# A four-layer graph network on one core: layer 1's inverse sums on ScalarE, its features by nodes, its first exponents inside layer 0

## The chip, the cores and the metric

The kernel runs on one core of a Trainium2 chip. A core has a tensor engine (PE) for matrix products and transposes, VectorE (DVE), ScalarE (ACT) and GpSimd (POOL), each with its own queue of instructions that it works through in order, and SyncE (SP), which issues DMAs here. PE writes to PSUM, eight banks of 2 KB a partition; everything else is in SBUF. The metric is device microseconds of one execution. The three runs before the change took 2126.72 us in the median (2126.08 to 2129.75).

## The reference, cut to what matters

Sixteen graphs share one adjacency matrix of 1024 nodes, each node has 64 features, and everything is float32. Four layers follow each other, each as `x = layernorm(x + layer(x))`. Layers 0 and 2 are graph attention with one score per edge, layer 3 has four heads. Layer 1, which the change is about, has a softmax of its own for each feature:

```python
feat = softplus(x * (INV_SQRT2 * w0) + b0)            # [16, 1024, 64]
scores = feat * wa + ba                               # wa, ba: one value per feature
logits = where(adj > 0, scores[:, None], -1e9)
attn = softmax(logits, axis=2)                        # over the neighbours j
out = einsum('bijd,bjd->bid', attn, feat)
x = layernorm(x + out)
```

Since the score depends on the neighbour alone, out is a quotient of two products with the adjacency matrix: adj @ (exp(score) * feat) over adj @ exp(score). The scores may be shifted by any constant per graph and feature, which cancels.

## The kernel before, in words

`fast_path` computes everything with shifts that fit ordinary data and collects tests of its bounds in `flags` (function `check`, L1750 to L1755). At the end a register is loaded from the smallest flag, and only if a test failed `general_path` computes everything again. One of the tests concerns `most_var`, the largest variance met in any layer norm, which is final only late in layer 3.

A node lies on partition p and in block c of 8 (`C`): x is held as `xg[g]`, [128 partitions, 8 blocks, 4 graphs, 64 features], for four groups g of four graphs. Two graphs side by side give 128 columns, a "pair"; q numbers the two pairs of a group.

**Layer 0** (`gat_layer`, L884 to L1142) works through the graphs in steps (b, k): batch b, node block k. At each step VectorE makes the weights `e` of one block (L964), PE multiplies those of four steps earlier (L976, L988), and further tasks hang on steps through the table `slots`: evictions, projections (L1016, L1020), division (L1033 to L1045), statistics, and the preparation of later graphs, whose product `pg` (L944) uses a PSUM pool `ps_g` with a single buffer of two banks. Tasks of other parts are hung on steps through the dictionary `extra`. The layer is issued under a manual schedule: each engine's order is the order written. What is outside such a block is ordered by the framework's planner, which fills in where it takes an engine to be idle: in the trace some of the checks (L1752, L1754) run in the middle of layer 0, and transposes of layer 2 (L903) among layer 1's products.

`gat_layer` returns the tasks left over at its end, `ending`: projection, division, residual, statistics, root and shift of batch 15, and the rows ("store") of batches 14 and 15, eight small ScalarE operations each (L775).

**Layer 1** follows (L1498 to L1607), outside a manual schedule. The adjacency is copied to `aR` in the type of the fast single-pass float32 product (L1512, eight casts). For each group, `prep_l1` makes the values. Per pair: eight transposes put features on partitions (L1522); ScalarE computes |z|, exp(-|z|), max(z, 0) and log(1+exp(-|z|)) (L1524 to L1528) and VectorE adds them (L1529): the softplus. Still with features on partitions, VectorE takes the maximum of feat*wa over the nodes (L1536) and from it the shift `down` (L1539), ScalarE makes the exponents (L1540), VectorE multiplies them by the features (L1541). Then both results are transposed back (`halves`, L1550, two times eight), and each is split in two numbers `hi` (a cast on ScalarE, L1552) and `lo` (the remainder, VectorE, L1553), so that two fast products give nearly full precision.

`product_l1` (L1567) forms for a group and a node block ic the sixteen products over the neighbours' blocks into one PSUM bank `po`, of a pool with two: quotient's numerator and denominator of both pairs. `average` (L1574 to L1582) divides and adds:

```python
nc.vector.reciprocal(r, po[:, :, 1, :])
nc.vector.tensor_tensor(r, po[:, :, 0, :], r, ALU.mult)
...
nc.vector.tensor_tensor(yf, r.rearrange("p q f -> p (q f)"), yf, ALU.add)
```

and takes the statistics of the layer norm. In the loop over groups (L1588 to L1607) each node block is followed by a task of the next group's preparation and one of the last group's normalization (`root`, `shift`, and `scaled` rows on ScalarE, 32 small operations a group). The preparation of group 0 runs before the first product, between the first three tasks of `ending`.

**The start**: SP's queue loads the first two graphs, the adjacency in eight pieces (four buffers), two more graphs, the weights of layers 2 and 3, the other twelve graphs, and then the six small pieces of layer 1's parameters `w0`, `b0`, `wa`, `ba`.

## Time and profile before

| What | Value |
|---|---|
| runs, median | 2126.72 us (2126.08 to 2129.75) |
| profiled execution | 2126.6 us, span 2124.7 us, mean PE clock 0.974 |
| layer 0's last product ends | 283.6 us |
| layer 1's products (L1567) | 308.5 to 448.3 us |
| busy in the span | PE 1998.2, VectorE 1858.1, ScalarE 1228.0, GpSimd 55.6 us |

The profile's page comes from one execution. A busy share is an average over stages that have different limits, so stretches of time and the chain of work that ended last have to be read beside it. In a row of groups, "mean ns of one" is the length of one instruction, and the last part tells how long its engine stood idle before it and what ended that. Rows of one engine overlap a little, so the spacing of starts is somewhat less than the length.

### The profile page before, as it was taken

The page shows a single profiled execution, that of the slowest core. Times are in us where ns is not written, and L with a number is a line of the kernel's source. Part 1 is how long each engine was busy: PE and PEld are TensorE (multiplying, and loading weights), DVE is VectorE, ACT ScalarE, POOL GpSimd, SP SyncE. Part 2 cuts the span into 40 slices and gives each one's busy share as a digit, 9 for nine tenths or more (in the row PEclk, how much of TensorE's full clock was granted, in tenths as well). Part 3 has the DMA queues.
Part 4 walks back from the last instruction along what each step waited for, and adds up shares of the span by engine and source line. Part 5 has one row for each costly group of instructions (what it writes and reads, how often), then busy time and mean ns, then how long its engine had stood idle before and what let it go on. Part 6 is the DMA issues. An engine that isn't in the chain of part 4 may idle for free.

```text
span 2124.7 us, 26159 instructions
## 1 busy us (share of the span) xinstructions
PE 1998.2 (94%) x10065; PEld 845.2 (40%) x10065; DVE 1858.1 (87%) x3224; ACT 1228.0 (58%) x1965; POOL 55.6 (3%) x77
## 2 busy tenths in 40 slices
PE   7999979988898999999999999999999999999993
PEld 3444447753332333333333333333333333333331
DVE  5888989989999867898888898889889889889997
ACT  4355566555556756556656655655665666565541
POOL 0000000000000000000000000000000000000001
PEclk7999989999989999999999999999999999999997
DMA  6000000000000100000000000000000000000000
GB/s 165 1 1 1 1 1 1 1 0 1 1 1 31 50 1 1 1 1 6 6 1 6 1 6 6 1 6 1 6 6 1 6 1 6 6 1 6 6 6 12
DMA packets 23654, 18.89 MB, mean 9 GB/s; under 512 B 19361, under 2 KB 19426, under 8 KB 23522
## 3 DMA queue, kind: packets, MB, share of 16 engines
q1 hardware_dynamic: 23218, 17.11, 2.7%
q8 instruction: 81, 1.33, 0.3%
q14 instruction: 51, 0.42, 0.1%
q10 hardware_dynamic: 304, 0.03, 0.0%
HBM read 12.95 MB, written 4.19 MB: 8 GB/s over the span
## 4 chain that ended last, share of the span: by engine, by line
PE 68%; DVE 26%; ACT 4%; issue 1%; DMA 0%; POOL 0%; SPq 0%; POOLq 0%; DVEq 0%; ACTq 0%
PE y L1293 19%; PE s L1281 17%; DVE e L964 7%; PE y_l L976 6%; PE s L1378 5%; PE y L1405 4%; DVE e L1286 4%; PE po L1310 3%; PE u_l L988 3%; PE po L1567 3%; ACT e L1285 1%; DVE r L1576 1%; PE pzT L1339 1%; PE phT L1255 1%; DVE junk L1396 1%
## 5 line engine op out<-in xcount | busy, mean ns | idle before, releaser
L1285 ACT ACTIVATE e<-s,shift 128x1024 f32<-128x1024 f32 x512 | 542.8, 1111 | 242.8 <-PE s L1281 237.4
L1286 DVE TENSOR_TENSOR e<-e,aT 128x1024 f32<-128x1024 f32 x512 | 602.5, 1220 | 87.2 <-ACT e L1285 85.1
L1281 PE MATMUL s<-hT 64*128 64x512 f32 x2048 | 508.9, 610 | 16.0 <-DVE top L1222 8.8
L1293 PE MATMUL y<-e,vals 128*64 128x512 f32 x2048 | 490.6, 601 | 3.2 <-ACT yT L1300 1.3
L964 DVE SCALAR_TENSOR_TENSOR e<-G_l,q,aT 128x1024 f32<-128x1024 f32 x256 | 315.4, 1278 | 7.2 <-ACT G_l L945 7.2
L976 PE MATMUL y_l<-e,vals_l 128*64 128x512 f32 x1024 | 263.6, 639 | 23.8 <-DVE e L964 23.0
L1281 PEld LDWEIGHTS s<-hT 64*128 64x128 f32 x2048 | 181.8, 186 | 256.3 <-issue 169.2
L1293 PEld LDWEIGHTS y<-e,vals 128*64 128x64 f32 x2048 | 131.0, 136 | 330.6 <-issue 257.7
L1383 ACT ACTIVATE e<-s,shift 128x1024 f32<-128x1024 f32 x128 | 141.7, 1112 | 84.8 <-PE s L1378 74.9
L1385 DVE TENSOR_TENSOR me<-e,aT 128x1024 f32<-128x1024 f32 x128 | 155.8, 1220 | 16.8 <-ACT e L1383 16.5
L1396 DVE SCALAR_TENSOR_TENSOR junk<-e,aN 128x1024 bf16<-128x1024 f32 x128 | 156.0, 1219 | 0.2
L1405 PE MATMUL y<-me,h2v 128*64 128x512 f32 x512 | 135.3, 609 | 10.6 <-DVE me L1385 10.4
L1378 PE MATMUL s<-h2T 64*128 64x512 f32 x512 | 136.3, 610 | 4.6 <-DVE h2v L1365 4.4
L976 PEld LDWEIGHTS y_l<-e,vals_l 128*64 128x64 f32 x1024 | 65.6, 142 | 162.2 <-issue 75.0
L1567 PE MATMUL po<-hi,aR 128*128 128x512 f32 x256 | 101.9, 398 | 2.7 <-ACT hi L1552 1.1
L1567 PE MATMUL po<-lo,aR 128*128 128x512 f32 x256 | 99.8, 390 | 0.0
L775 ACT ACTIVATE x<-m,bn_shift,bn_rstd 128x64 f32<-128x64 f32 x256 | 88.2, 429 | 0.0
L1340 ACT COPY zT<-pzT 128x1024 f32<-128x1024 f32 x32 | 32.4, 1013 | 78.4 <-PE pzT L1339 78.4
L1310 PEld LDWEIGHTS po<-wb,yT 128*128 128x128 f32 x512 | 62.0, 190 | 34.0 <-issue 21.1
L1310 PE MATMUL po<-wb,yT 128*128 128x130 f32 x512 | 73.8, 287 | 1.3 <-ACT e L1285 1.2
L1378 PEld LDWEIGHTS s<-h2T 64*128 64x128 f32 x512 | 46.6, 186 | 63.7 <-issue 41.4
L1405 PEld LDWEIGHTS y<-me,h2v 128*64 128x64 f32 x512 | 32.7, 137 | 93.8 <-issue 56.1
(214 smaller groups left out, 2003.7 us busy)
## 6 DMA issues: line engine op xcount, KB each, us to landing
adj<-in_adj_dram SPq DMA_DIRECT2D x16, 512.0 KB, 4.5
x<-in_x_dram SPq DMA_DIRECT2D x16, 256.0 KB, 5.0
out_dram<-res SPq DMA_DIRECT2D x16, 256.0 KB, 2.0
wl<-in_L_gnn_Wh_dram SPq DMA_DIRECT2D x2, 64.0 KB, 4.8
wo<-in_L_gnn_Wo_dram SPq DMA_DIRECT2D x1, 64.0 KB, 4.4
l_wd<-in_L_gnn_W_dram ACTq DMA_DIRECT2D x2, 16.0 KB, 4.7
l_wd<-in_L_gnn_W_dram SPq DMA_DIRECT2D x2, 16.0 KB, 2.1
bo<-in_L_gnn_bo_dram SPq DMA_DIRECT2D x1, 32.0 KB, 3.1
```

The costliest lines, as they stand in the source:

```text
L964: nc.vector.scalar_tensor_tensor(e, G[b - b % 2][:, b % 2, :], pq[b - b % 2][1][:, k, b % 2 : b % 2 + 1], aT[:, k, :], ALU.max, ALU.mult,)
L976: nc.tensor.matmul(held["y"][h * D : (h + 1) * D, :], vals[b][:, k, :], e[:, h * HALF : (h + 1) * HALF], start=(k == 0), stop=(k == C - 1),)
L1281: nc.tensor.matmul(s[:, i, :], hT[rows, k * P : (k + 1) * P], hT[rows, cols], start=True, stop=True)
L1285: nc.scalar.activation(e, s, AF.Exp, bias=shifts[b, n])
L1286: nc.vector.tensor_tensor(e, e, bc_mid(aT[:, k, cols], 2), ALU.mult)
L1293: nc.tensor.matmul(held[h][i * D : (i + 1) * D, :], vals[b][:, k, :], e[:, i, :], start=(k == 0), stop=(k == C - 1),)
L1310: nc.tensor.matmul(o[:, j // 2, j % 2, :], held["y"][:, c * P : (c + 1) * P], wb[:, n, :], start=True, stop=True,)
L1378: nc.tensor.matmul(s[:, i, :], hT[rows, (i + k // CH) % 2, k % CH * P : (k % CH + 1) * P], hT[rows, 0, :], start=True, stop=True,)
L1385: nc.vector.tensor_tensor(m, e, aT[:, k, :].rearrange("p (i q) -> p i q", i=2), ALU.mult)
L1396: nc.vector.scalar_tensor_tensor(junk, held.pop(k).rearrange("p i q -> p (i q)"), 1.0, aN[:, k, :], ALU.mult, ALU.mult, accum_out=sums[:, ...
L1405: nc.tensor.matmul(held["o"][h * D : (h + 1) * D, :], vals["out", b][:, k, :], e[:, h, :], start=(k == 0), stop=(k == C - 1),)
L1567: nc.tensor.matmul(po.rearrange("p q k f -> p (q k f)"), aR[:, k, ic * P : (ic + 1) * P], e[:, k].rearrange("p q k f -> p (q k f)"), start ...
```

## The change

Four things change. First, in `average` the reciprocal is replaced: ScalarE takes the logarithm of the denominator and the exponential of its negative, VectorE corrects that by a Newton step (two operations), multiplies, and subtracts, since the step leaves the sign turned. `r1` gets two buffers, `t1` is new. The headroom of layer 1's exponents goes from 60 to 30, and a test of a new bound (`spread`, made from the parameters) is added.

Second, the softplus is computed with nodes on partitions, straight from `xg`. One set of transposes (`turn`) brings it to features on partitions for the exponents, which read it from PSUM; the exponents alone are transposed back, and the product with the features is made in the nodes' layout (`back`, `weighted`). So a pair needs two sets of eight transposes in place of three.

Third, the parameters are loaded and prepared in `first`, ahead of the loads of the later graphs, and the first seven tasks of group 0's two pairs are hung on steps (7, 0) to (12, 5) of layer 0. Their tiles lie in a pool of their own, and the transposes use layer 0's `ps_g`. Before the first product remain `back` and `weighted` of both pairs, three tasks of `ending`, and the casts of `aR`, now half on ScalarE.

Fourth, all tests share one buffer.

```diff
+    def layer1_weights():
+        w0 = row_bc(L1_w0.rearrange("a b -> (a b)"), 1, "w0")
+        l1["b0"] = row_bc(L1_b0, 1, "b0")
+        for k, ap in (("wa", L1_wa), ("ba", L1_ba)):
+            l1[k] = const.tile([P, 1], F32, tag=k, name=k)
+            for i in range(2):
+                nc.sync.dma_start(l1[k][i * D : (i + 1) * D, :], ap.unsqueeze(1))
+        l1["c0"] = const.tile([P, 1], F32, tag="c0", name="c0")
+        nc.vector.tensor_scalar(l1["c0"], w0, INV_SQRT2, None, ALU.mult)
+        spread = const.tile([P, 1], F32, tag="spread", name="spread")
+        nc.vector.memset(spread, 1.0)
+        for k, n in (("c0", D**0.5), ("b0", 1.0), ("wa", None)):
+            size = small.tile([P, 1], F32, tag="size", name="size")
+            nc.vector.scalar_tensor_tensor(size, l1[k], -1.0, l1[k], ALU.mult, ALU.max)
+            if n:
+                nc.vector.scalar_tensor_tensor(spread, size, n, spread, ALU.mult, ALU.add)
+            else:
+                nc.vector.tensor_tensor(spread, spread, size, ALU.mult)
...
+    def prep_l1(g, q):
+        x = xg[g][:, :, 2 * q : 2 * q + 2, :].rearrange("p c b d -> p c (b d)")
+        def size():
+            h["t"] = l1["pool"].tile([P, C, P], F32, tag="t", name=f"t{g}_{q}")
+            nc.scalar.activation(h["t"], x, AF.Abs, bias=l1["b0"], scale=l1["c0"])
+        def decay():
+            nc.scalar.activation(h["t"], h["t"], AF.Exp, scale=-1.0)
+        def above():
+            h["f"] = l1["pool"].tile([P, C, P], F32, tag="f", name=f"f{g}_{q}")
+            nc.scalar.activation(h["f"], x, AF.Relu, bias=l1["b0"], scale=l1["c0"])
+        def log():
+            nc.scalar.activation(h["t"], h["t"], AF.Ln, bias=1.0)
+        def feature():
+            nc.vector.tensor_tensor(h["f"], h["f"], h["t"], ALU.add)
+        def turn():
+            h["pf"] = l1["psum"]("pf")
+            for c in range(C):
+                nc.tensor.transpose(h["pf"][:, c, :], h["f"][:, c, :], ident)
+        def exponents():
...
+            nc.vector.tensor_scalar(t, pf, wa, None, ALU.mult, ALU.max, accum_out=top)
+            nc.vector.tensor_tensor(top, top, ba, ALU.add)
...
+            nc.vector.scalar_tensor_tensor(down, ba, HEADROOM_1, top, ALU.add, ALU.subtract)
+            nc.scalar.activation(t, pf, AF.Exp, bias=down, scale=wa)
+        def back():
...
+            for c in range(C):
+                nc.tensor.transpose(pe[:, c, :], t[:, c, :], ident)
+            hi, lo = his[g][:, :, q, 1, :], los[g][:, :, q, 1, :]
+            nc.scalar.copy(hi, pe)
+            nc.vector.tensor_tensor(h["f"], h["f"], pe, ALU.mult)
+            nc.vector.tensor_tensor(lo, pe, hi.bitcast(F32), ALU.subtract)
+        def weighted():
+            hi, lo = his[g][:, :, q, 0, :], los[g][:, :, q, 0, :]
+            nc.scalar.copy(hi, h["f"])
+            nc.vector.tensor_tensor(lo, h["f"], hi.bitcast(F32), ALU.subtract)
+        return [size, decay, above, log, feature, turn, exponents, back, weighted]
...
+                layer1_weights()
                 for b in range(4, B):
                     load_x(b)
...
+        l1_tasks = [prep_l1(0, q) for q in range(2)]
         extra = {(0, 6): [lambda: gat_setup(later["w2"], "l2", True)], (1, 2): [lambda: later["w3"]()]}
+        for q, todo in enumerate(l1_tasks):
+            t = 7 + 2 * q
+            places = (t, 0), (t, 2), (t, 4), (t, 6), (t + 2, 2), (t + 2, 7), (t + 3, 5)
+            for place, task in zip(places, todo):
+                extra.setdefault(place, []).append(task)
...
         def average(g, ic, po, st):
-            r = l1.tile([P, 2, P], F32, tag="r1", name="r1", bufs=1)
-            nc.vector.reciprocal(r, po[:, :, 1, :])
-            nc.vector.tensor_tensor(r, po[:, :, 0, :], r, ALU.mult)
+            r = pool.tile([P, 2, P], F32, tag="r1", name="r1", bufs=2)
+            nc.scalar.activation(r, po[:, :, 1, :], AF.Ln)
+            nc.scalar.activation(r, r, AF.Exp, scale=-1.0)
+            t = pool.tile([P, 2, P], F32, tag="t1", name="t1", bufs=1)
+            nc.vector.tensor_tensor(t, po[:, :, 1, :], r, ALU.mult)
+            nc.vector.scalar_tensor_tensor(r, t, 2.0, r, ALU.subtract, ALU.mult)
+            nc.vector.tensor_tensor(t, po[:, :, 0, :], r, ALU.mult)
...
-            nc.vector.tensor_tensor(yf, r.rearrange("p q f -> p (q f)"), yf, ALU.add)
+            nc.vector.tensor_tensor(yf, yf, t.rearrange("p q f -> p (q f)"), ALU.subtract)
...
-        for i, todo in enumerate(prep_l1(0)):
-            for task in todo + ending[i : i + 1] * (i < 3):
-                task()
+        for i, task in enumerate([l1_tasks[q][-2 + i] for q in range(2) for i in range(2)]):
+            for k in range(2 * i, 2 * i + 2):
+                (nc.scalar.copy if k % 2 else nc.vector.tensor_copy)(aR[:, k, :], aT[:, k, :])
+            for todo in [task] + ending[i : i + 1] * (i < 3):
+                todo()
...
+            for q in range(2 if g + 1 < NG else 0):
+                for ic, task in zip((q, q, q, q, q + 1, q + 2, q + 2, q + 4, q + 5), prep_l1(g + 1, q)):
+                    ahead[ic].append(task)
...
-        t = small.tile([P, ap.shape[1]], F32, tag=f"ok{len(ok)}", name="ok", bufs=1)
+        t = small.tile([P, B * (H + 1) * C], F32, tag="ok", name="ok", bufs=1)[:, : ap.shape[1]]
...
+    check(l1["spread"], ALU.is_le, MOST_SPREAD)
```

## The prediction

> **What bounds the kernel now.** I read the page first (PE busy 94%, VectorE 87%), then stretches of the span, because the shares do not say which engine limits layer 1. Columns: length, busy time of each engine, granted clock, DMA share, GB/s.
>
> ```profile
> core 0: us, PE busy (x) PEld busy (x) DVE busy (x) ACT busy (x) POOL busy (x), PEclk, DMA share, GB/s
> ...
> 180.00:220.00 40.00, 40.00 (x278) 17.41 (x276) 36.81 (x87) 22.30 (x64) 1.24 (x1) 1.00 0.00 1
> ...
> 283.50:308.50 25.00, 11.09 (x76) 10.11 (x72) 20.49 (x47) 18.46 (x26) 0.00 (x0) 0.66 0.00 0
> ...
> 345.00:380.00 35.00, 33.86 (x174) 27.88 (x173) 34.29 (x82) 25.93 (x48) 0.00 (x0) 1.00 0.01 1
> 380.00:415.00 35.00, 33.80 (x171) 27.58 (x169) 34.69 (x79) 24.97 (x47) 0.00 (x0) 1.00 0.00 1
> 415.00:448.10 33.10, 32.82 (x145) 26.77 (x144) 31.01 (x80) 12.22 (x35) 0.00 (x0) 1.00 0.00 1
> ```
>
> Layer 0 (to 283.5) is limited by PE: 40.00 of 40. Then come 25 us in which PE works 11, at a clock of 0.66. In layer 1's groups 0 to 2 VectorE is fullest (34.3 and 34.7 of 35), with PE just behind; in group 3, which prepares no successor, it is PE. The chain that ended last says the same: nearly all VectorE up to 419, then PE.
>
> ```profile
> 407.56 1.66 DVE r L1576
> 409.22 1.08 DVE lo L1553
> ...
> 419.09 29.27 PE po L1567 x128
> ```
>
> So the eight products of a group take 29.3 us of PE, 3.66 each. From the first product (308.55) to 419.09 three groups took 110.5 us, 36.8 each. The groups of that stretch give VectorE's price for one node block:
>
> ```profile
> L1576 DVE RECIPROCAL r<-po 128x256 f32<-128x256 f32 x31 | 54.1, 1746 | 4.8 <-PE po L1567 4.6
> ...
> L1580 DVE TENSOR_TENSOR x<-r,x 128x256 f32<-128x256 f32 x31 | 13.1, 423 | 0.6
> L1577 DVE TENSOR_TENSOR r<-po,r 128x256 f32<-128x256 f32 x31 | 13.0, 418 | 0.4
> L1552 ACT CAST hi<-pe 128x1024 fp32r<-128x1024 f32 x12 | 12.1, 1009 | 19.5 <-PE pe L1550 19.5
> ```
>
> And the order of time shows the gap between the layers: transposes at half speed (1.94 for eight; 1.03 later), products held by the last `hi`.
>
> ```profile
> 298.23 1.94 PE L1550 MATMUL pe<-ident,r 128*128 128x128 f32 x8 [10.73 <-DVE r L1541]
> ...
> 308.55 0.50 PE L1567 MATMUL po<-hi,aR 128*128 128x512 f32 x1 [1.10 <-ACT hi L1552]
> ```
>
> **1. The gap between the layers, -11.1.** Softplus, exponents and half of the transposes of group 0 leave it. What stays after layer 0's last product (283.6), from the spacings of the rows:
> VectorE: 4 casts of `aR` at 0.63 (eight are done by 288.6 now), `f*pe` 2 x 1.14, `lo` 4 x 1.1, and the divide (1.05) and residual (1.4) of batch 15, which stand between them: 2.5 + 2.3 + 4.4 + 2.45 = 11.7.
> ScalarE: the other 4 casts, 4 `hi` copies at 0.95, batch 13's or 14's rows (8 x 0.335 = 2.7) and batch 15's exponential 0.6. The nearest row for a cast on ScalarE is L817's copy of the same shape out of PSUM: 1.01 on ScalarE, 0.69 on VectorE. Sum 4 + 3.8 + 2.7 + 0.6 = 11.1.
> About 12.2 with the first transposes. Here the Trainium skill speaks against the change: "ScalarE: Activation LUTs", Rules for kernel authors, gives simple pointwise work to VectorE, as the faster engine per element. The rows agree on the engines (0.69 against 1.01). By the rule all eight casts stay on VectorE: 11.7 + 2.5 = 14.2 for the gap. By the rows, two full engines side by side end at about 12.2. I take 12.2, as both lists are independent.
> PE's clock: it stood at 0.50 from 290 and rose at about 307, three us after PE restarted at 304.0. Today those slow us lie behind waiting; afterwards the last transposes come early, PE idles up to the first product, and the products' first 3.4 us run at half speed: +1.7. The gap goes from 25.0 to 13.9. Bounds: 12.2 (clock stays up) and 22 (ScalarE is given other work first, below).
>
> **2. The averages, -6.9.** VectorE now: 1.75 + 0.42 + 0.42 + 0.60 (statistics), in spacings 3.05. After: four 256-wide operations (0.43 each, a dependent one can't overlap) and the statistics 0.57 = 2.3. "VectorE: DVE Perf Modes", Rules for kernel authors, says of chained operations to keep their count down; this change adds one. By that rule alone the block costs about 0.43 more, 3.5, and the stage grows by 24 x 0.43 = 10 us; by the rows it loses a 1.75 and gains two of 0.43. The reciprocal costs 6.8 ns an element and the others 1.6, so the row decides: -0.75 a block, 6 a group.
> ScalarE gets a logarithm and an exponential, 128x256. No row has that width; between 0.23 (128x32, L702) and 0.59 (128x512, L999) lies 0.40, so 0.7 for the pair back to back, 5.6 a group. Bounds 0.23 and 0.59 each. The preparation keeps its seven passes: L1540 from SBUF with a bias and a scale takes 1.24, L1524 from PSUM 1.21, so exchanging sources changes nothing. ScalarE had 25 to 26 of 35, 27.2 of a 36.8 group; after, 32.8.
> PE: 8 x 3.66 + four instead of six sets of eight transposes, 0.93 each = 33.0. VectorE: 35.3 - 6 = 29.3.
> So PE leads at 33.0 with ScalarE at 32.8. Today the period is 1.5 over its fullest engine (36.8 against 35.3); I keep that: 34.5, three times -2.3 = -6.9. Bounds: 33.0 (-11.4) and 36.8 (0).
> New waits: VectorE's first multiplication waits for ScalarE's exponential, and behind it on VectorE stand the `lo` and softplus additions for the next group. On ScalarE the logarithm waits for the product, and behind it stand `hi` copies, which the next group's products need, but a group later. Two `acc` banks: a block's way L from its last matmul to the release of its bank may last 2 x 4.1 - 3.66 = 4.6 us before PE stalls (4.1 = 33.0/8). I make L 0.4 + 0.4 + 3 x 0.43 + 0.3 for handovers + one foreign operation of about 0.6 on each engine = 3.6.
> After the very last product L replaces the reciprocal: 0.3 + 0.8 + 1.7 + 0.57 = 3.4 against 3.1 now: +0.3.
>
> **3. Moved into layer 0, +1.9.** PE is full there, so its two sets of transposes cost 2 x 0.93. VectorE: addition 1.14, maximum 1.20 and two tiny ones, 2.5 per pair of batches prepared. It has this row's idle time per two batches (30.8 us):
>
> ```profile
> 175.60 0.17 DVE L1033 TENSOR_SCALAR l_sums<-po 128x8 f32<-128x8 f32 x1 [2.27 <-PE po L1020]
> ```
>
> so the cover is 2.5 and just suffices; without it up to 5.0. ScalarE: five passes of about 1.1, twice, in some 18 idle us per 40. Its exponential waits for VectorE's `down`; behind it stand layer 0's evictions, which PE needs two to four products later. The features of q = 0 borrow the one `g` buffer from (9,7) to (10,5), between its uses at (9,3) and (10,7); if they keep it two places too long, `pg` waits, whose result is needed nine places later. Costs 0 each, together at most 5.
>
> **4. Setup, +0.5.** Six small DMAs move on SP's queue, ahead of the loads of x from batch 4 on. They take 4.4 us there now (37.75 to 42.1); those loads start at 28.5 instead of 24.2 and land 5 later, and their first reader is a transpose at 59.6: cover 26 us. The scaling moves earlier and seven small VectorE operations are new (0.15 each, 1 us), in a phase where VectorE is busy 22 of 34; a wait for a small DMA in its queue would hold the first batches. 0 to 2, I take 0.5.
>
> **5. The checks, +0.5.** They now share one buffer, so all but the first queue behind that of `most_var`, at 2055:
>
> ```profile
> 2055.12 0.18 DVE L1752 TENSOR_SCALAR ok<-most_var 128x32 f32<-128x32 f32 x1
> ...
> 2060.00:2070.00 10.00, 7.10 (x38) 2.93 (x34) 7.55 (x17) 1.40 (x2) 0.00 (x0) 1.00 0.02 5
> 2070.00:2080.00 10.00, 8.54 (x44) 4.03 (x44) 8.49 (x16) 6.01 (x8) 0.35 (x1) 1.00 0.06 24
> ```
>
> Four of 0.29 + 0.41, two of 0.18 + 0.28 and the new one (0.33) make 4.05 us. Layer 2, where VectorE is busy 58.7 of 60, loses 1.9 of that. The tail gains all 4.05 unless they fall into the 4.0 that VectorE idles from 2060 to 2080. Between -1.9 and +2.2 (4.05 - 1.9); half in the gaps gives 0.1 to 0.5, I take 0.5.
>
> **Sum**: -11.1 - 6.9 + 0.3 + 1.9 + 0.5 + 0.5 = -14.8. The profiled execution took 2126.6 with a span of 2124.7, 1.9 around it; the median of the runs is 2126.72, the same. 2124.7 - 14.8 = 2109.9, with 1.9: **2112**.
>
> **Rivals.**
> A, the sum: 2112, by its bounds 2107 to 2117. Chance 0.62.
> B, ScalarE becomes the bound of groups 0 to 2: it needs 32.8 of 33.0 by my count, its idle times today are waits for PE (19.5 for `hi`), and it can't be late without holding a bank. Then the stage gains nothing: 2112 + 6.9 = 2119. For it: three engines near full. Against: group 0 scales only half as many rows. 0.16.
> C, the gap stays long: ScalarE's queue gets layer 0's rows and group 1's softplus ahead of the `hi` copies (a row pass of 2.76 already stands ahead of the first `t` at 284.2). 22 instead of 13.9: 2120. 0.09.
> D, all fits: the gap 12.2 without loss of clock, groups at 33.0, the checks in idle slots: -12.8 - 11.4 + 0.3 + 1.9 - 1.9 = -23.9, 2103. 0.08.
> E, slower: the release of `acc`. If other operations slip between the chained ones (a 1.14 stands between reciprocal and multiplication today) at each of five places, L passes 4.6 and PE runs at (3.66 + L)/2 per block. At L = 5.5 the stage is as today (4.6 a block); the whole change breaks even at +14.8 over 24 blocks on 4.31, 4.93 a block, L = 6.2, and is 0.2% slower at L = 6.5. At L = 7: 5.33 a block, 24 x 1.02 = 24.5 more, 2136. Against: VectorE has slack there. 0.04.
> F, the new bound fails and the whole is computed again by the other path: from the reference's weights it is (1 + 8 x 1.727 + 1.296) x 2.727 = 43.9, below 60. Without it the multiple of the time. 0.01.
>
> **How the numbers follow.** 0.2% is 4.25 us, about what a measurement of this kernel tells from no change. Faster (below 2122.5): A 0.61, D 0.08, B 0.13, C 0.06 = 0.88. Same: what B, C and A leave above, 0.07. Slower 0.05 (E, F). The range takes A whole, B, most of C and part of D: 2104 to 2121.
>
> **What would show it.** Right: first product about 14 us after layer 0's last; no reciprocal of 1.7; VectorE near 30 and ScalarE near 32 per 35 us of groups 0 to 2; these at 34 to 35 us each; layer 0 two us longer. Wrong: PE waiting for VectorE's release of `po` in groups 1 and 2, a `hi` copy late behind softplus in the gap, VectorE idle for a small DMA before 50, or a dense run of checks after 2080.

## The result, and the profile after

| | median | runs | ratio to before, 95% interval |
|---|---|---|---|
| before | 2127.18 us | 16 | |
| changed | 2119.76 us (2117.16 to 2128.50) | 16 | 0.9967 [0.9954, 0.9979] |
| changed, second series | 2119.80 us (before beside it: 2129.58) | 6 | 0.9953 [0.9937, 0.9969] |

The change makes the kernel 7.4 us faster, 9.8 us in the second series. The forecast was 14.8 us less, 2112 us. The direction held and the time lies within the range, but half of the gain is missing.

The first profiled execution of the changed kernel took 2117.32 us, with a span of 2115.4 us. It can be cut where the same instruction stands in both traces: the 17th weight block of layer 0, the last product of layer 0, the first and last product of layer 1, the first and 121st weight block of layer 2, the 17th and 625th exponential of layer 3, and the end. The lengths in us:

| stretch | before | after | difference | forecast |
|---|---|---|---|---|
| start, to the 17th weight block | 65.75 | 64.64 | -1.11 | +0.5 |
| on to layer 0's last product | 217.87 | 219.73 | +1.86 | +1.9 |
| gap to layer 1's first product | 24.93 | 12.50 | -12.43 | -12.8 |
| layer 1's products | 139.80 | 137.07 | -2.73 | -5.2 (averages -6.9, slow clock +1.7) |
| on to layer 2's first weights | 10.69 | 11.21 | +0.52 | +0.3 |
| layer 2, to its 121st | 208.18 | 207.57 | -0.61 | -1.9 |
| crossing into layer 3 | 50.07 | 50.03 | -0.04 | |
| layer 3 | 1326.70 | 1326.62 | -0.08 | |
| end | 80.76 | 86.08 | +5.32 | 0 to +4.05 |
| sum | 2124.75 | 2115.45 | -9.30 | |

Two stretches vary from one execution to the next: over the twelve profiled executions of the changed kernel and its variants below, the start takes 64.6 to 71.2 us and the crossing 50.0 to 53.1 us. A second profile of the unchanged program (`e12_after`) is 8.0 us longer than the first: 4.64 us of that lie at the start, 3.08 us in the crossing, 0.3 us in all the rest. So experiments are compared below by the sum of the other seven stretches, called the **inner sum**: 2008.93 us before, 2000.78 us after, 8.15 us less.

The busy time by stretches of the changed kernel, with the columns that the prediction explained:

```profile
core 0: us, PE busy (x) PEld busy (x) DVE busy (x) ACT busy (x) POOL busy (x), PEclk, DMA share, GB/s
180.00:220.00 40.00, 40.00 (x276) 17.78 (x268) 39.31 (x88) 24.89 (x66) 1.24 (x1) 1.00 0.00 1
284.40:296.90 12.50, 3.88 (x41) 3.56 (x41) 10.66 (x18) 12.46 (x20) 0.00 (x0) 0.81 0.00 1
296.90:303.70 6.80, 6.76 (x17) 4.87 (x18) 4.08 (x15) 6.17 (x6) 0.00 (x0) 0.59 0.00 0
335.90:370.70 34.80, 32.98 (x161) 27.48 (x162) 29.55 (x90) 29.66 (x62) 0.00 (x0) 1.00 0.00 1
370.70:404.80 34.10, 32.93 (x162) 27.28 (x161) 29.20 (x91) 23.03 (x57) 0.00 (x0) 1.00 0.01 1
404.80:434.00 29.20, 29.14 (x129) 23.80 (x127) 20.19 (x79) 16.63 (x51) 0.00 (x0) 1.00 0.00 1
```

VectorE in layer 0 went from 36.81 to 39.31 of 40. In the gap ScalarE works 12.46 of 12.50. The first product follows at a clock of 0.59 and takes 6.76 us (4.80 before). In groups 1 and 2 (the next two rows) VectorE has room now, and PE is fullest.

The groups of instructions of groups 1 and 2 show what replaced the reciprocal:

```profile
L1633 DVE BATCH_NORM_STATS2 st<-x 128x6 f32<-128x64 f32 x65 | 9.9, 214 | 0.4
...
L1627 DVE SCALAR_TENSOR_TENSOR r<-t,r 128x256 f32<-128x256 f32 x16 | 6.8, 424 | 0.3
...
L1626 DVE TENSOR_TENSOR t<-po,r 128x256 f32<-128x256 f32 x16 | 6.7, 418 | 5.5 <-ACT r L1624 5.5
L1624 ACT ACTIVATE r<-r 128x256 f32<-128x256 f32 x15 | 6.2, 415 | 0.2
L1623 ACT ACTIVATE r<-po 128x256 f32<-128x256 f32 x15 | 5.7, 380 | 7.2 <-PE po L1613 7.1
```

The logarithm takes 380 ns and the exponential 415 ns, where the prediction read 0.40 us off two other widths. The groups last 39.05, 34.76, 34.08 and 29.17 us from start to start; before, 36.98, 37.16, 36.41 and 29.26 (the last of each to the end of its last product).

At the end of the kernel, VectorE in order of time (start, length, line; the last bracket is idle time and what ended it):

```profile
2040.48 0.17 DVE L1811 TENSOR_SCALAR ok<-most_var 128x32 f32<-128x32 f32 x1
...
2041.29 0.29 DVE L1811 TENSOR_SCALAR ok<-l_s 128x256 f32<-128x256 f32 x1
2041.62 0.42 DVE L1813 TENSOR_REDUCE flags<-ok 128x1 f32<-128x256 f32 x1
2041.95 1.21 DVE L1290 TENSOR_TENSOR e<-e,aT 128x1024 f32<-128x1024 f32 x1
2043.09 0.29 DVE L1811 TENSOR_SCALAR ok<-l_s 128x256 f32<-128x256 f32 x1
...
2048.28 0.29 DVE L1813 TENSOR_REDUCE flags<-ok 128x1 f32<-128x128 f32 x1
...
2056.39 0.69 DVE L1428 TENSOR_TENSOR v<-po,rt 128x512 f32<-128x512 f32 x1 [3.57 <-PE po L1422]
```

The checks stand between the last weight blocks of layer 3 (L1290), which PE waits for. VectorE had no room there: before the change, the stretch in which the check of `most_var` ran (at 2055.12 us) was this, in the view of busy time by stretches:

```profile
2050.00:2060.00 10.00, 8.83 (x44) 3.30 (x42) 9.83 (x17) 5.93 (x8) 0.00 (x0) 1.00 0.00 0
```

PE of the changed kernel, in order of time:

```profile
2051.62 3.68 PE L1297 MATMUL y<-e,vals 128*64 128x512 f32 x8 [3.95 <-DVE e L1290]
2055.24 1.12 PE L1422 MATMUL po<-ident,y2T 128*128 128x128 f32 x4
```

PE stood 3.95 us, its clock fell within that pause (at 2050.1 us, for 6.8 us), and VectorE in turn stood 3.57 us for L1422.

### The profile page after: what moved, and what is told of

It reads as the page before. It is cut to its first block, busy times and chain, and to the rows that moved or that the text cites. A ratio compares the mean times of both kernels' runs of the same rounds, so it can differ in the third digit from the quotient of the medians.

```text
span 2115.4 us, 26176 instructions
## 1 busy us (share of the span) xinstructions
PE 1991.2 (94%) x10001; PEld 837.8 (40%) x10001; DVE 1832.3 (87%) x3261; ACT 1252.5 (59%) x2033; POOL 56.5 (3%) x77
## 4 chain that ended last, share of the span: by engine, by line
PE 69%; DVE 23%; ACT 5%; issue 1%; DMA 0%; POOL 0%; SPq 0%; POOLq 0%; DVEq 0%; ACTq 0%
PE y L1297 19%; PE s L1285 17%; DVE e L968 7%; PE y_l L980 6%; PE s L1382 5%; PE y L1409 4%; DVE e L1290 4%; PE po L1613 4%; PE po L1314 3%; PE u_l L992 3%; ACT e L1289 1%; ACT x L779 1%; PE phT L1259 1%; PE pzT L1343 1%; PE pg L948 1%
## 5 line engine op out<-in xcount | busy, mean ns | idle before, releaser
L1290 DVE TENSOR_TENSOR e<-e,aT 128x1024 f32<-128x1024 f32 x512 | 602.4, 1219 | 87.6 <-ACT e L1289 85.5
L1389 DVE TENSOR_TENSOR me<-e,aT 128x1024 f32<-128x1024 f32 x128 | 155.7, 1219 | 16.8 <-ACT e L1387 16.5
L1409 PE MATMUL y<-me,h2v 128*64 128x512 f32 x512 | 135.3, 609 | 10.5 <-DVE me L1389 10.4
```

The costliest lines, as they stand in the source:

```text
L1290: nc.vector.tensor_tensor(e, e, bc_mid(aT[:, k, cols], 2), ALU.mult)
L1389: nc.vector.tensor_tensor(m, e, aT[:, k, :].rearrange("p (i q) -> p i q", i=2), ALU.mult)
L1409: nc.tensor.matmul(held["o"][h * D : (h + 1) * D, :], vals["out", b][:, k, :], e[:, h, :], start=(k == 0), stop=(k == C - 1),)
```

## The experiments

Each edit is to the changed kernel, except in `e2_before_shared`. "Inner" is the difference of the inner sum to the changed kernel's first profile (for `e2_before_shared` to that of before). The kernel before, run beside them, had a median of 2127.82 us beside e1 to e4, 2127.67 beside e5 to e8, 2128.55 beside e9 and e10 and 2129.58 beside the last two.

| run | median us | ratio to before, 95% | inner us |
|---|---|---|---|
| e1_order | 2117.69 | 0.9954 [0.9940, 0.9967] | -4.44 |
| e2_before_shared | 2132.28 | 1.0021 [1.0012, 1.0030] | +4.84 |
| e3_warm | 2121.93 | 0.9971 [0.9960, 0.9981] | -0.53 |
| e4_late0 | 2128.70 | 1.0005 [0.9999, 1.0012] | +7.46 |
| e5_oldavg | 2125.89 | 0.9990 [0.9982, 0.9998] | +4.03 |
| e6_pool | 2129.37 | 1.0007 [1.0001, 1.0014] | +7.30 |
| e7_fused | 2115.97 | 0.9949 [0.9936, 0.9963] | -5.33 |
| e8_warm18 | 2118.41 | 0.9967 [0.9956, 0.9978] | -1.08 |
| e9_spread | 2118.72 | 0.9951 [0.9937, 0.9965] | -1.62 |
| e10_hold | 2143.23 | 1.0064 [1.0047, 1.0080] | +18.26 |
| e11_best | 2114.46 | 0.9936 [0.9919, 0.9952] | -6.22 |
| e12_after | 2119.80 | 0.9953 [0.9937, 0.9969] | +0.30 |

**The end: is it the checks?** Two runs, one that moves a check, one that puts the shared scratch alone into the kernel before.

```diff
     check(adj_low, ALU.is_le, 0.0)
-    check(most_var, ALU.is_le, MOST_VAR)
     check(l1["spread"], ALU.is_le, MOST_SPREAD)
...
+    check(most_var, ALU.is_le, MOST_VAR)
     check(sums.rearrange("p b h c -> p (b h c)"), ALU.is_ge, LEAST_SUM)
```

> The changed kernel with one thing moved: the check of most_var stands last but one, so that the shared scratch of the checks is not held by it and the checks of layers 0 and 2 can run early, as in the kernel before. Theory (the end is lost to the checks that pile up behind most_var on VectorE and let TensorE's clock fall): the end of layer 3 gets back the 5.75 us that it lost, layer 2 gives up about 0.6 us again, so some 5 us less than the changed kernel: profiled time near 2112 us, ratio to before 0.993; TensorE's clock stays at 1.0 from 2035 us to 2080 us. Rival (the end is slower for another reason, as the chains of layer 3 start at another phase): within 1.5 us of the changed kernel, 2116 to 2119 us profiled, ratio 0.997, and the clock falls again near 2050 us.

The end takes 80.76 us, exactly as before the change (86.08 with it). The four wide checks run early again, as their row says (least, median and greatest ns, then first and last start):

```profile
L1811 DVE TENSOR_SCALAR ok<-l_s x4: 279/288/293, 234.9 to 632.1; 128x256 f32<-128x256 f32 x4
```

The busy time in the stretch where the changed kernel's clock fell (columns as above), first of the changed kernel, then of this one:

```profile
2040.00:2050.00 10.00, 6.31 (x28) 2.16 (x28) 9.62 (x27) 5.22 (x6) 0.00 (x0) 1.00 0.00 0
2050.00:2060.00 10.00, 6.79 (x27) 3.63 (x28) 5.69 (x13) 0.59 (x1) 0.00 (x0) 0.66 0.00 1
```

```profile
2040.00:2050.00 10.00, 8.84 (x44) 3.30 (x42) 9.83 (x17) 5.92 (x8) 0.00 (x0) 1.00 0.01 2
2050.00:2060.00 10.00, 7.10 (x40) 2.95 (x36) 7.54 (x17) 1.33 (x2) 0.00 (x0) 1.00 0.01 2
```

PE works 8.84 of 10 in place of 6.31, and the clock stays at 1.00. The theory holds for the end and the clock. The ratio of 0.993 was not reached: the median moved by 2.1 us only. The stretches that vary, the start and the crossing, were 2.3 and 1.5 us longer in this profile than in the changed kernel's first one; the inner sum shows 4.44 us.

```diff
-        t = small.tile([P, ap.shape[1]], F32, tag=f"ok{len(ok)}", name="ok", bufs=1)
+        t = small.tile([P, B * (H + 1) * C], F32, tag="ok", name="ok", bufs=1)[:, : ap.shape[1]]
```

> The kernel before with one thing of the change alone: the checks share one scratch buffer, in their order of before. Theory (shared scratch makes them wait for most_var): the six checks of layers 0 and 2 run after 2050 us, the end is 4 to 6 us later, ratio 1.0020 to 1.0028. Rival (their place costs nothing, the end of the changed kernel is lost to something else): ratio 1.000 or below, as layer 2 is freed of some 4 us of VectorE.

The end grows from 80.76 to 86.29 us, layer 2 shrinks from 208.18 to 207.17 us, and the median is 4.5 us longer, with an interval wholly above 1. So the shared scratch, with `most_var` second in the order, costs this by itself.

**One instruction for two in each check.** To see what the checks cost in their early places; this comes on top of the edit of `e1_order`:

```diff
-        nc.vector.tensor_scalar(t, ap, bound, None, op)
         r = flags[:, len(ok) : len(ok) + 1]
-        nc.vector.tensor_reduce(r, t, AX.X, ALU.min)
+        nc.vector.tensor_scalar(t, ap, bound, None, op, ALU.min, accum_out=r)
```

> As e1_order, and each check made by one instruction (comparison and minimum along the row in one pass, the result written as its accumulated value) in place of two: 0.37 us for 0.70 us of each of the four wide checks. Theory (the checks of layers 0 and 2, back in their early places, cost what VectorE spends on them there, some 1.7 us in layer 2 and 0.7 us behind layer 0): 1.0 to 1.4 us less than e1_order from the end of layer 0 to the start of layer 3, ratio 0.9948 to 0.9950. Rival (VectorE has room for them there and the loss of e1_order in layer 2 is one of the order of instructions): within 0.3 us of e1_order in these stretches.

From layer 0's last product to the crossing's end this kernel takes 420.53 us, `e1_order` 420.79 us: the rival holds. The estimate was wrong in part because one such pass with its accumulated minimum is slower than a plain one: 418 + 82 ns for each wide check in place of 288 + 420 ns, 0.2 us less where 0.33 us were expected. The rows of the wide checks in this kernel, as above:

```profile
L1812 DVE TENSOR_SCALAR_CACHE_REDUCE ok<-l_s x4: 409/418/419, 234.1 to 630.9; 128x256 f32<-128x256 f32 x4
L1812 DVE DVE_READ_ACCUMULATOR ok<-l_s x4: 80/82/82, 234.5 to 631.2; 128x1 f32 x4
```

The end, with `most_var`'s and the last check shorter, takes 80.18 us.

**The move.** Group 0's features and exponents issued behind layer 0, as before:

```diff
-        for q, todo in enumerate(l1_tasks):
-            t = 7 + 2 * q
-            places = (t, 0), (t, 2), (t, 4), (t, 6), (t + 2, 2), (t + 2, 7), (t + 3, 5)
-            for place, task in zip(places, todo):
-                extra.setdefault(place, []).append(task)
...
-        for i, task in enumerate([l1_tasks[q][-2 + i] for q in range(2) for i in range(2)]):
+        q0, q1 = l1_tasks
+        for i, part in enumerate([q0[:5], q1[:5], q0[5:7], q1[5:7] + q0[7:8], q0[8:], q1[7:8], q1[8:]]):
```

> The changed kernel with the move undone: group 0's features and exponents are made behind layer 0, as before; averages, features by nodes and checks stay. Theory (the move is worth the forecast 11.1 us less the 1.9 us that it costs in layer 0): layer 0 ends 1.9 us earlier, the gap to the first product is 21 to 25 us for 12.5 us, so the end of layer 1 is 7 to 10 us later and the time near 2125 us profiled, ratio 0.9995 to 1.001. Rival (most of the gap is the wait for layer 0's own end, and the move is worth little): end of layer 1 within 3 us of the changed kernel.

The size is near the theory's: the inner sum grows by 7.46 us, the median by 8.9 us. The end of layer 1 comes 5.9 us later (7 to 10 were expected), and 2.0 us more are lost ahead of layer 2. But the gap is 16.5 us, not 21 to 25, and layer 0 is not shorter (220.33 us): it has 16 transposes less, but also 3.41 us at half clock from 162.7 us on, after a pause of 0.71 us. The trace of this kernel says why the gap is short. ScalarE, in order of time:

```profile
111.23 1.24 ACT L1509 ACTIVATE t<-x,b,c 128x1024 f32<-128x1024 f32 x1
...
148.91 1.06 ACT L1519 ACTIVATE t<-t 128x1024 f32<-128x1024 f32 x1
```

Although they are written behind layer 0, the planner put all eight passes of group 0's softplus into layer 0, at 111 to 150 us, since they need nothing but x. Only transposes, maximum and exponents were left behind (16 transposes at 287.93 us, the exponentials at 292.5 and 294.6 us). So the part of the move that the planner can't make by itself shortens the gap by 4.0 us and lets the first product start at a less slow clock (6.76 us for 8.18 us). The other 8.4 of the gap's 12.4 us come with the features by nodes, with fewer transposes and with the casts on two engines; how much each brings was not taken apart. That the planner could move the softplus because it no longer holds a PSUM bank is a reading of the program, not tested.

**The new average.** The old one put back:

```diff
-            nc.scalar.activation(r, po[:, :, 1, :], AF.Ln)
-            nc.scalar.activation(r, r, AF.Exp, scale=-1.0)
...
+            nc.vector.reciprocal(r, po[:, :, 1, :])
+            nc.vector.tensor_tensor(r, po[:, :, 0, :], r, ALU.mult)
...
-            nc.vector.tensor_tensor(yf, yf, t.rearrange("p q f -> p (q f)"), ALU.subtract)
+            nc.vector.tensor_tensor(yf, r.rearrange("p q f -> p (q f)"), yf, ALU.add)
```

> The changed kernel with the old average: VectorE's reciprocal and two operations on it in place of logarithm, exponential and the Newton step; all else of the change stays. Reading of the changed kernel's trace (the new average is worth some 2.4 us in each of groups 1 and 2, and 0.5 us in group 0, where stalls took the rest): groups 1 and 2 last 36.5 to 37.2 us each for 34.8 and 34.1, the end of layer 1 is 5 to 5.5 us later, time near 2125 us, ratio 0.9990. The forecast's own step (2.3 us in each of the three groups): 6.6 us later, near 2126.4 us. Rival (the average does not set the pace, the gain of layer 1 is all from the move): within 1 us of the changed kernel, 2119 to 2121 us.

The groups last 37.88, 35.79, 37.38 and 30.89 us, the products 141.94 us for 137.07: +4.87. The reading of the trace holds in its sum (5 to 5.5 were expected), not group by group, and in the sum partly by chance. Groups 2 and 3 each begin with 3.41 us at half clock, which the changed kernel does not have there, right behind a pause of PE for the release of a bank. The first of the two, PE in order of time and then the stretch in the view of busy time:

```profile
374.17 0.68 PE L1613 MATMUL po<-hi,aR 128*128 128x512 f32 x1 [1.92 <-DVE r L1628]
```

```profile
374.25:377.66 3.41, 3.41 (x9) 2.64 (x10) 3.41 (x9) 3.41 (x4) 0.00 (x0) 0.50 0.02 5
```

The second pause is 2.27 us, with half clock from 411.80 us on. The first products of these groups take 5.49 and 5.50 us, the second ones 3.79 us each, so that some 3.4 of the 4.87 us are the slow clock's, and 1.5 us remain for the average itself (an estimate from these figures). Whether each execution has these two stretches, no other profile shows. The forecast's own 6.6 us is too high, and the rival is out for the whole, though without the slow clock it would have been close.

**Why the groups stall.** In the changed kernel 2.69 us pass between the products of blocks 7 and 8 and 2.67 us between those of blocks 14 and 15, in every profile of this order (blocks counted from 0 through the layer). In each, PE works 0.9 us on eight transposes and then stands idle, for 1.81 and 1.79 us; the expectations below call the whole 2.7 us a pause. VectorE in order of time, at the average of block 5 of the changed kernel:

```profile
326.74 0.42 DVE L1626 TENSOR_TENSOR t<-po,r 128x256 f32<-128x256 f32 x1 [0.18 <-ACT r L1624]
327.19 0.42 DVE L1627 SCALAR_TENSOR_TENSOR r<-t,r 128x256 f32<-128x256 f32 x1
327.64 1.22 DVE L1549 TENSOR_TENSOR f<-f,pe 128x1024 f32<-128x1024 f32 x1
328.78 0.42 DVE L1628 TENSOR_TENSOR t<-po,r 128x256 f32<-128x256 f32 x1
329.11 1.22 DVE L1550 TENSOR_TENSOR lo<-pe,hi 128x1024 fp32r<-128x1024 f32 x1
330.24 0.41 DVE L1631 TENSOR_TENSOR x<-x,t 128x256 f32<-128x256 f32 x1
330.58 1.22 DVE L1522 TENSOR_TENSOR f<-f,t 128x1024 f32<-128x1024 f32 x1
```

Between the four chained operations of one average stand passes of 1.22 us. L1549 and L1550 belong to group 1's values; L1522 already to group 2's features, which the planner starts a group early, as their inputs are ready. At blocks 6 and 7, which follow, a bank is held 6.64 and 5.96 us after the product's last matmul, 2.3 us at a calm block. The average of block 6, with two wide passes in it (L1533 is the maximum for group 2's exponents):

```profile
332.23 0.41 DVE L1626 TENSOR_TENSOR t<-po,r 128x256 f32<-128x256 f32 x1
332.55 1.22 DVE L1555 TENSOR_TENSOR lo<-f,hi 128x1024 fp32r<-128x1024 f32 x1
333.68 0.42 DVE L1627 SCALAR_TENSOR_TENSOR r<-t,r 128x256 f32<-128x256 f32 x1
334.15 1.28 DVE L1533 TENSOR_SCALAR_CACHE_REDUCE t<-pf,wa 128x1024 f32<-128x1024 f32 x1
...
335.36 0.42 DVE L1628 TENSOR_TENSOR t<-po,r 128x256 f32<-128x256 f32 x1
```

L1628 releases the bank at 335.78 us, and block 8, which takes it, starts right behind. PE in the same view (the tiny operation that it names, L1534, ended just after the release):

```profile
335.92 0.47 PE L1613 MATMUL po<-hi,aR 128*128 128x512 f32 x1 [1.81 <-DVE top L1534]
```

Three runs look for what to change.

Two of VectorE's five wide passes of a half on GpSimd:

```diff
-            nc.vector.tensor_tensor(h["f"], h["f"], h["t"], ALU.add)
+            nc.gpsimd.tensor_tensor(h["f"], h["f"], h["t"], ALU.add)
...
-            nc.vector.tensor_tensor(lo, h["f"], hi.bitcast(F32), ALU.subtract)
+            nc.gpsimd.tensor_tensor(lo, h["f"], hi.bitcast(F32), ALU.subtract)
```

> The changed kernel with two of the four wide passes of each half of the preparation (the sum of the features, and the low half of the weighted features, both from SBUF to SBUF) on GpSimd in place of VectorE: 4.8 us of VectorE's time less in each group. Theory (TensorE's stalls at blocks 5 to 8 and 13 to 15 come from these passes, which stand in VectorE's queue between the four operations of an average): the pauses of 2.7 us ahead of blocks 8 and 15 go, groups 0 to 2 last 33 to 33.8 us but for the slow clock in group 0, the end of layer 1 is 3 to 4 us earlier, ratio 0.9945 to 0.9950. Rival (the pauses come from ScalarE's place in the chain, its logarithm waiting behind its own wide passes, or GpSimd's passes are so long that the halves come late): groups as long as before or longer, end of layer 1 0 to 6 us later.

The rival holds, and by more than it said: the groups take 41.05, 38.45 and 34.75 us, and the end of layer 1 comes 7.7 us later (0 to 6 were expected). GpSimd needs twice VectorE's 1.21 us for a pass, as the Trainium skill has it for operations with two inputs ("GPSIMD Engine Reference", Engine selection). Its groups in this kernel:

```profile
L1522 POOL TENSOR_TENSOR f<-f,t 128x1024 f32<-128x1024 f32 x8 | 21.0, 2628 | 24.2 <-issue 17.6 <-ACT t L1519 5.2 <-ACT f L1516 1.4
L1555 POOL TENSOR_TENSOR lo<-f,hi 128x1024 fp32r<-128x1024 f32 x8 | 20.0, 2506 | 137.2 <-ACT hi L1554 137.2
```

VectorE's part at block 7 falls from 5.03 to 2.96 us, but there the logarithm waits 1.72 us behind other work of ScalarE (0.12 us without the edit). So the pauses come not from VectorE alone.

The last steps of the first half one block earlier:

```diff
-                for ic, task in zip((q, q, q, q, q + 1, q + 2, q + 2, q + 4, q + 5), prep_l1(g + 1, q)):
+                for ic, task in zip((q, q, q, q, q + 1, q + 2, q + 2, 3 + 2 * q, 4 + 2 * q), prep_l1(g + 1, q)):
```

> The changed kernel with the last steps of the next group's preparation at other blocks: back and weighted of the first half at blocks 3 and 4 for 4 and 5, those of the second half at 5 and 6 as before. In the changed kernel's trace blocks 5 and 6 hold, beside their averages, two backs, two weighteds and the planner's early start on the features of the group after the next: VectorE takes 4.4 and 5.0 us from the exponential to the release there, for 1.4 us elsewhere. Theory (the pauses of 2.7 us ahead of blocks 8 and 15 are this heap of wide passes, too many for two blocks and not too many for the group): with them apart, the pauses shrink to under 1 us, groups 0 to 2 are 1.5 to 2.5 us shorter each, 4 to 6 us in all, ratio 0.9940 to 0.9948. Rival (ScalarE and VectorE are as full as the group lets them be; the heap moves to other blocks): groups within 0.7 us of 39.1, 34.8 and 34.1, ratio 0.996 to 0.997.

Between the two: the idle times ahead of blocks 8 and 15 are gone, and PE's idle time within the products falls from 5.0 to 1.8 us. The groups take 37.45, 35.09 and 33.01 us, the products 134.78 us, 2.3 less, of which 0.8 is lost again ahead of layer 2.

The early start taken away:

```diff
+            h["b"] = small.tile([P, 1], F32, tag="b0g", name=f"b0g{g}_{q}") if g else l1["b0"]
+            if g:
+                nc.vector.scalar_tensor_tensor(h["b"], l1["st"][:, q * GB, :1], 0.0, l1["b0"], ALU.mult, ALU.add)
-            nc.scalar.activation(h["t"], x, AF.Abs, bias=l1["b0"], scale=l1["c0"])
+            nc.scalar.activation(h["t"], x, AF.Abs, bias=h["b"], scale=l1["c0"])
```

> The changed kernel with the early start taken away: the bias of the features of groups 1 to 3 is made anew by one small operation that reads a statistic of the block that they are written behind (its value times 0, plus the bias), so that they can't be moved ahead of it; the places stay as they are. Theory (the early start of the features of the group after the next, with two of the wide passes and up to eight of ScalarE's passes, is what overfills blocks 5 and 6): pauses ahead of blocks 8 and 15 under 1 us, groups 1 to 2 us shorter, ratio 0.9945 to 0.9955. Rival (it is the two backs and weighteds themselves, all at blocks 4 to 6; the early start used time that was free): groups as long or up to 3 us longer, as the features now crowd blocks 0 to 3, ratio 0.997 to 0.999.

Neither: the groups take 44.96, 40.55 and 40.59 us, six us more each. ScalarE in order of time in group 0 of this kernel (its lines stand three further down), where block 1's last matmul ends at 312.61 us:

```profile
312.80 1.25 ACT L1512 ACTIVATE t<-x,b0g,c 128x1024 f32<-128x1024 f32 x1
313.95 1.23 ACT L1519 ACTIVATE f<-x,b0g,c 128x1024 f32<-128x1024 f32 x1
315.09 1.04 ACT L1515 ACTIVATE t<-t 128x1024 f32<-128x1024 f32 x1
316.04 0.36 ACT L1626 ACTIVATE r<-po 128x256 f32<-128x256 f32 x1
```

L1626 is the logarithm here. It waits 3.43 us behind three passes of the features, and the bank is held for 7.24 us. This is the mechanism of the prediction's case E. With the passes at these places the new average pays only because the planner starts the features a group early and so spreads ScalarE's passes: without that the products take 155.28 us, 15.5 us more than before the change. Other places were not tried.

**The slow first product.** Matmuls whose result is overwritten, put on PE in the gap; 12 of them, then 18:

```diff
-            for k in range(C):
-                for e in (his[g], los[g]):
+            fill = FILL if (g, ic) == (0, 0) else 0
+            for k, e in [(0, None)] * fill + [(k, e) for k in range(C) for e in (his[g], los[g])]:
```

> The changed kernel with 12 matmuls of fp32 (256 columns, result overwritten) put on TensorE ahead of layer 1's first product, while it waits for the halves. Theory (the clock falls in the idle gap and the first products pay for it): the clock stays at 1.0 through 303 us, the first product takes 3.7 to 4 us for 6.8 us, the end of layer 1 is 2 to 3 us earlier, ratio 0.9955. Rival (the slow first product is hidden, as the averages of the first blocks set the pace, or 12 are too few to hold the clock): end of layer 1 within 0.5 us of the changed kernel.

> As e3_warm with 18 matmuls for 12 (8.0 us for 5.3 us at the 445 ns that one took there), so that TensorE pauses for less than 1 us ahead of layer 1's first product; with 18 the order of some instructions in group 0 is another as well. In e3_warm the pause was 3.4 us and the clock still fell, 1.7 us after TensorE had begun again. Theory (a pause of 3.4 us is enough for the clock to fall, one of under 1 us is not): the clock stays at 1.0 from 290 us to 312 us, the first product takes 3.7 to 4.0 us for 6.3 us, group 0 lasts 36 to 37 us for 38.6 us, the end of layer 1 comes 2 us earlier against the end of layer 0. Rival (the clock falls all the same, or the averages of the first blocks hide it): group 0 lasts 38 us or more.

With 12, PE pauses from 299.84 to 303.28 us, 3.44 us, and the clock still falls, but after PE has gone on. Busy time and clock by stretches of `e3_warm`:

```profile
303.30:305.30 2.00, 1.48 (x5) 0.89 (x6) 1.97 (x8) 2.00 (x3) 0.00 (x0) 0.92 0.00 0
305.30:308.30 3.00, 3.00 (x9) 2.32 (x8) 2.12 (x8) 3.00 (x4) 0.00 (x0) 0.50 0.00 0
```

A clock (the third number from the end) of 0.92 over 2 us is full clock up to 305.0 us and half clock after it. The first product takes 6.31 us and the products gain 0.5 us, so that the rival holds: 12 are too few. With 18 the pause is 0.85 us and the clock holds, in the same view of `e8_warm18`:

```profile
290.00:296.00 6.00, 5.93 (x28) 4.88 (x26) 6.00 (x7) 6.00 (x8) 0.00 (x0) 1.00 0.00 1
296.00:302.00 6.00, 4.69 (x19) 3.60 (x20) 4.80 (x18) 6.00 (x7) 0.00 (x0) 1.00 0.00 0
```

The first product takes 4.73 us (3.7 to 4.0 were expected), group 0 36.95 us for 39.05, the products 2.1 us less: the theory holds but for the first product. Ahead of layer 2 0.8 us of it is lost, so that 1.1 to 1.3 us remain, too little for the median to show. These numbers contain another order of some instructions in group 0.

The Trainium skill ("TensorE: Matmul & The Clock Gate", Part 1) says that the clock is halved after an idle window of some 3.4 us, and that this window runs free of the kernel. Pauses of 8.62 us (changed kernel, gap), 3.95 us (its end) and 3.44 us (`e3_warm`) came with a fall, the one of 0.85 us did not. But the runs don't bear out 3.4 us as a limit: those of 1.92 and 2.27 us in `e5_oldavg` came with a fall too, those of 1.81 and 1.79 us in the changed kernel did not.

The traces' clock records show more. In all fourteen, each stretch at one clock lasts a whole multiple of 3.41 us, on one grid through the trace. Cut into the windows of this grid (from 70 us on, without the last 25 us), the traces have 113 windows at full clock in which PE was busy, transposes included, for less than 45% of the time. All 113 were followed by half clock, and of the 7931 fuller ones 48 were. In `e3_warm` the window from 301.57 to 304.99 us held half of the pause, PE was busy for 35% of it, and the clock fell at its end. So where a pause lies on the grid counts beside its length; no run moved a pause to test this.

**Together, and once more.**

> The changed kernel with the gains of e7_fused (most_var's check last but one, each check one instruction), e8_warm18 (18 matmuls in the pause ahead of layer 1) and e9_spread (the first half's last two steps a block earlier) together. Theory (they lie in different stretches, so they add up): e7_fused's 2115.97 us less 1.3 us of the warm start and 1.4 us of the spread steps, 2113.3 us, ratio 0.9935; no more than 6 us of pauses ahead of layer 1's blocks. Rival (the order that the planner makes in group 0 is another with the three together and stalls elsewhere): 2115 us or more.

> The changed kernel itself once more, beside e11_best on the same chip. Theory (its profiled execution came out 1 to 5 us shorter than most, as the start up to 65 us differs by up to 6.5 us from one execution to the next with the same program, and the clock's fall behind layer 2 is met in some only): median near 2119.8 us, its profile differs from the first one's mostly in front of 65 us and between 670 and 700 us, and not in layer 1 nor in the end. Rival (the first profile is the rule, the median of the first runs was of a disturbed chip): median 2117 to 2118 us.

`e11_best` takes 2114.46 us, 5.3 us less than the changed kernel beside it (2119.80 us), the fastest of all. Its gain is mostly the checks'. The two edits of layer 1 don't add: the products take 135.24 us, no less than with either alone (134.98, 134.78), with group 0 at 38.08 us and PE idle for 0.6, 1.9 and 1.6 us ahead of blocks 7, 8 and 16. Here the rival was right about the cause, and the time lies between the two.

`e12_after` agrees with its theory: the same median as the first series, and the stretches as told above. The start and the crossing of two executions of one program, in the view of busy time by stretches, first the first profile and then this one:

```profile
662.00:702.00 40.00, 36.44 (x184) 13.19 (x180) 35.08 (x77) 31.77 (x57) 1.06 (x3) 1.00 0.34 106
20.00:65.00 45.00, 35.68 (x190) 16.44 (x188) 30.96 (x80) 20.35 (x51) 1.37 (x1) 0.82 0.42 79
```

```profile
662.00:702.00 40.00, 36.44 (x177) 12.93 (x174) 33.84 (x75) 29.48 (x51) 0.70 (x2) 0.96 0.25 79
20.00:65.00 45.00, 36.97 (x156) 16.14 (x155) 29.06 (x75) 17.88 (x41) 1.37 (x1) 0.66 0.42 81
```

At the start the granted clock is 0.82 in the one and 0.66 in the other, and PE gets fewer instructions done. Two profiles of the kernel before and with its shared scratch have a crossing of 50.07 and 50.06 us; of the twelve of the changed kernel and its variants three have 50.0 to 50.1 us and nine 51.5 us or more. Whether the change makes the longer crossing more frequent stays open.

## Why the prediction was wrong where it was

The likeliest case, A, named -14.8 us, against -7.4 us (medians), -9.3 us (spans) and -8.15 us (inner sum). Of its steps:

**1, the gap: right.** -12.43 us in the gap and +1.96 us in the first product, together -10.5 for -11.1; half clock reached 5.6 us into the products where 3.4 us were assumed. ScalarE bounds it (12.46 of 12.50), at 1.03 us a cast for VectorE's 0.68: of the two that the prediction weighed, all casts on VectorE or two engines side by side, the rows speak for the second, though closely. With all casts on VectorE its 10.66 would be some 13.2 us, an estimate from these rows, for 12.5; no run had them there. The row of the Trainium skill that was weighed against this ("ScalarE: Activation LUTs", Rules for kernel authors) names `relu`, `max`, `min`, `add` and `mul`, and no cast. What was wrong is the reason: the step credited the move with the softplus's leaving, and `e4_late0` shows that the planner takes it out of the gap by itself.

**2, the averages: right for two groups, wrong for one.** Groups 1 and 2 last 34.8 and 34.1 us for the 34.5 forecast, 2.4 and 2.3 us less than before for 2.3. The mean time to the release of a bank in them is 3.60 us for 3.6; that this mean hit is partly luck, as it ranges from 2.2 to 7.1 us. The step failed where it gave the same 2.3 us to group 0. That group takes 39.05 us for 36.98. About 2.0 us of this is the slow first product, and with the clock held (`e8_warm18`) it takes 36.95 us: PE works 1.7 us less in it than before, with fewer transposes, and stands idle 1.7 us more (2.54 us for 0.84), mostly in the 1.8 us ahead of block 8. So the stage gained 4.7 us by the traces (2.73 + 1.96), not 6.9. The step took one mean foreign operation per block; the planner gives some blocks none and others two wide ones on VectorE and one or two on ScalarE, and PE waits behind the full ones.

Nor is the gain the average's alone. With the old average (`e5_oldavg`) group 1, at full clock in all three kernels, takes 35.79 us, between 37.16 before and 34.76: of its 2.4 us, 1.4 come with the rest of the change and 1.0 with the average. That `e5_oldavg` gives 4.9 us, near 4.7, is chance, as 3.4 of it are the slow clock's.

**3, moved into layer 0: right.** +1.86 us for +1.9, and PE is busy for all of the 219.73 us, with 16 transposes more than before.

**4, setup: can't be read.** Its 0.5 us is less than the start's variation of 6.6 us.

**5, the checks: wrong, and the largest miss.** +5.32 us at the end and -0.61 us in layer 2 make +4.7 for +0.5. The step had seen that the checks would queue behind that of `most_var`, and had priced their 4.05 us rightly. It failed where it put half of them into the 4.0 idle us of VectorE from 2060 to 2080 us. They are ready as soon as `most_var`'s check is done, and so ran right there, in the row of 10 us in which VectorE was busy 9.83 before (shown with the result). And it left out what follows: PE, kept 3.95 us from its next weights, fell to half clock for 6.8 us, so that 4.05 us of work cost 5.3. `e1_order` and `e2_before_shared` show both, from either side. Nor did layer 2 give back 1.9 us when it lost the checks: 0.6 and 1.0 us.

The misses are 4.2 us in step 5, 2.2 in step 2 and 0.6 in step 1, together 7.0; with the start's -1.1 for +0.5, the crossing and layer 3 that is the difference of the spans, -9.3 for -14.8, to 0.3 us. Some 2 us more separate the profiled execution from the median, and the variation of the start and the crossing is of that size.

Of the rivals, B (ScalarE becomes the bound) gave the time that was nearest to the measured one, 2119 us, and is refuted as a cause: ScalarE works 29.66 and 23.03 us in groups of 34.8 and 34.1 us, and the average's gain is there. C is out (gap 12.5 us), D too. E was not met, but `e10_hold` shows it one dependency away.

## What to carry to other kernels

A scratch tile that several operations share puts them in the order of the one that is ready last: place that one last, or keep buffers apart, and price such a heap at the place where it becomes ready, not in the next idle stretch. What one engine's heap costs is more than its own length once PE's wait lets its clock fall; so look at the granted clock in both kernels before a difference is put down to the edit. Where a planner orders the work, undoing a move in the program may not undo it on the engines: read from the trace where the instructions ran.

## What the runs showed of the hardware

- The clock's fall can come after the pause: in `e3_warm` it came at 305.0 us, 1.7 us after PE had ended its pause, and lasted 3.4 us. A pause may be paid for by products that come behind it.
- In these traces the clock changed on a grid of 3.41 us only, and all 113 windows at full clock with PE busy for less than 45% were followed by half clock. A pause of 1.92 us came with a fall, one of 1.81 us did not.
- GpSimd's sum or difference of 128x1024 fp32 took 2.63 and 2.51 us for VectorE's 1.21 us.
- A comparison with its minimum accumulated took 418 + 82 ns for 256 columns, the plain comparison 288 ns and the minimum after it 420 ns.
- Two executions of one program agreed to 0.25 us in each stage but two; the first 65 us differed by 4.6 us (by up to 6.6 us over all variants) and the crossing into layer 3 by 3.1 us.
